# Seven late weight loads in a pairwise-product kernel: from SyncE's queue over sixteen DMA engines to GpSimd's queue over fourteen

## The chip, the cores and the metric

The kernel runs on one core of a Trainium2 chip. The core has TensorE (PE, with its weight loads as PEld), VectorE (DVE), ScalarE (ACT), GpSimd (POOL), SyncE (SP), and sixteen DMA engines that move data between HBM and the core's memory. The metric is device time in microseconds (us); the kernel before takes 754.85 us, the median of three runs (754.69 to 755.86).

## The reference

There are 1024 samples with 32 fields of 128 numbers each. Every pair of fields i < j (496 pairs) has a 128 x 128 matrix of its own:

```python
v_i = inputs[:, I_IDX, :]
v_j = inputs[:, J_IDX, :]
transformed = jnp.einsum('bpd,ped->bpe', v_i, W)
return transformed * v_j
```

All of it is float32. The output is 1024 x 496 x 128 numbers, 260 MB; the inputs are 17 MB of fields and 32 MB of matrices.

## The kernel before

**Layout and order.** The host transposes, so that the embedding dimension lies on the 128 partitions and the samples run along the free dimension. The pairs go from i = 30 down to i = 0, and for each i over j = i+1 to 31. A unit u is half a pair (512 samples); two units make a pair q, two pairs a chunk c, eight pairs one weight load (`WL`), four pairs one output group (`OG`). The order of all instructions on each engine is the order in which the Python loop over u (L215) writes them out; the scheduler doesn't move them. An engine that waits therefore holds up all that the loop wrote for it later.

**One unit.** The first 15 pairs use one float32 matmul each (L188). All others use three matmuls on split operands: the field and the matrix are each cut into a high part, a rest and a correction. `first(u)` issues two matmuls (L191) and a scaling of the result in PSUM by ACT (L192); three units later `second(u)` adds the third matmul (L200), and VectorE multiplies the result by field j into the output tile (L206). Eight PSUM tiles hold units in flight.

**Splitting.** For a chunk of two matrices ACT makes the high part (`wh`, L110), and GpSimd then makes `wl` and `wd` in three operations (L111 to L113). The same is done for each field in two halves (L125 to L131; for the first fields the last of these operations is VectorE's, L238). A chunk's split is written out three chunks ahead of its use and has four buffers. The list `todo` gives at most one such task a pair.

**Weights.** A weight load is one tile of 128 partitions by 4 KB (512 KB), three such tiles in turn (`WB`). Load c holds chunks 4c to 4c+3 and is issued on SP's queue (`load_w`, L98 to L101). It may start when the last split of load c-3, that of chunk 4c-9, has been read. Its place in the loop is pair 8c-17 (`w_at`, L158 to L162; 8c-11 for loads 55 to 57), but SP has next to nothing else to do and gets there early: it issues when the tile comes free.

**Fields.** Fields 17 to 31 have tiles of their own. Fields 1 to 16 lie in four tiles of 16 KB a partition (`g0` to `g3`), loaded four fields at a time by SP (L91 to L96). Field 0 comes late into one of the weight tiles.

**Output.** A group of four pairs fills one 16 KB tile, which ACT's queue stores as one DMA of 2 MB (L231). There are three such tiles of their own, and until their fields are loaded the four tiles `g0` to `g3` serve too (`out_tile`, L171 to L175). From the load of `g0`, at 473.6 us of the profile, on only the three are left. VectorE can't start a group before the store that last used its tile has landed. The last groups are stored in smaller pieces.

**Queues.** SP's queue carries the loads, ACT's queue the stores and four early loads. GpSimd issues no DMA.

Of the kernel before, what the change touches and what calls it, by code (L numbers as in the profile page):

```python
# [7 lines left out]
F32 = mybir.dt.float32  # L8
# [3 lines left out]
P = 128  # L12
# [5 lines left out]
WL = 8  # L18
# [9 lines left out]
XLEAD = 5  # L28

XG = 4  # L30
XWAIT = 12
OWAIT = 20
SLAG = 2
# [8 lines left out]
def kernel(  # L42
# [22 lines left out]
    nc = tc.nc  # L65
# [3 lines left out]
    xpool = ctx.enter_context(tc.tile_pool(name="x", bufs=1))  # L69
# [8 lines left out]
    def load_x(f, pieces=1, eng=None):  # L78
        if f == 0:

            t = rpool.tile([P, WL, P], F32, tag="w", name="x_0").rearrange("p q e -> p (q e)")
        else:
            t = xpool.tile([P, BT], F32, tag=f"x{f}", name=f"x_{f}")
        s = BT // pieces
        for k in range(pieces):
            (eng or nc.sync).dma_start(out=t[:, k * s : (k + 1) * s], in_=xt[f, :, k * s : (k + 1) * s])
        x_sb[f] = t

    w_raw = {}

    def load_group(k):  # L91
        t = xpool.tile([P, XG, BT], F32, tag=f"g{k}", name=f"x_g{k}")
        f = XG * k + 1
        nc.sync.dma_start(out=t, in_=xt[f : f + XG].rearrange("m d b -> (m d b)").rearrange("(d m b) -> d m b", m=XG, b=BT))
        for m in range(XG):
            x_sb[f + m] = t[:, m, :]  # L96

    def load_w(c, splits=(0, WL), eng=nc.sync):  # L98
        w_raw[c] = rpool.tile([P, WL, P], F32, tag="w", name=f"w_{c}")
        for a, b in zip(splits, splits[1:]):  # L100
            eng.dma_start(out=w_raw[c][:, a:b, :], in_=wt[c, :, a:b, :])  # L101

# [30 lines left out]
    nq0 = NATIVE * (NATIVE + 1) // 2  # L133
# [11 lines left out]
    todo.sort(key=lambda t: t[1])  # L145

    load_w(0, (0, 1, WL), nc.sync)
    load_x(NF - 2, pieces=2, eng=nc.scalar)
    load_x(NF - 1, pieces=2, eng=nc.scalar)
    load_x(NF - 3)  # L150
    load_x(NF - 4)
    load_w(1, eng=nc.sync)
    for f in range(NF - 5, NF - 4 - XLEAD, -1):
        load_x(f)
    load_w(2, eng=nc.sync)


    w_at = {}  # L158
# [4 lines left out]
    x_at = XAFTER * WL - 11  # L163
    assert x_at not in w_at and len(w_at) == NQ // WL - WB

    ngroup = NF // XG // 2
    group_at = {first_q[XG * k + XG + 1] - XWAIT: k for k in range(ngroup)}
    until = {f"g{k}": q - OWAIT for q, k in group_at.items()}
# [12 lines left out]
    def first(u):  # L181
        q, h = divmod(u, 2)
        i, c = pairs[q][0], q // WC
        r = slice(q % WC * P, (q % WC + 1) * P)
        s = slice(h * HB, (h + 1) * HB)
        po[u] = ppool.tile([P, HB], F32, tag="po", name=f"po_{u}")
        if q < nq0:
            nc.tensor.matmul(po[u], w_raw[q // WL][:, q % WL, :], x_sb[i][:, s], start=True, stop=True)  # L188
        else:
            for t in (0, 1):  # L190
                nc.tensor.matmul(po[u], w_s[c][t][:, r], x_s[i][t][:, s], start=t == 0, stop=t == 1)  # L191
            nc.scalar.mul(po[u], po[u], 1.0 + EPS)  # L192

    def second(u):
        q, h = divmod(u, 2)
        i, j = pairs[q]
        r = slice(q % WC * P, (q % WC + 1) * P)
        s = slice(h * HB, (h + 1) * HB)
        if q >= nq0:
            nc.tensor.matmul(  # L200
                po[u], w_s[q // WC][2][:, r], x_s[i][2][:, s], start=False, stop=True, skip_group_check=True
            )
        g, k = divmod(q, OG)
        if k == 0 and h == 0:
            ots[g] = out_tile(g)
        nc.vector.tensor_tensor(ots[g][:, k, s], po.pop(u), x_sb[j][:, s], ALU.mult)  # L206
        if q >= NQ - 2:
            stores.append((u + SLAG, out[g, :, k, s], ots[g][:, k, s]))
        elif g == 0 or q >= NQ - OG:
            if h == 1:  # L210
                stores.append((u + SLAG, out[g, :, k], ots[g][:, k]))
        elif k == OG - 1 and h == 1:
            stores.append((u + SLAG, out[g], ots[g]))

    for u in range(2 * NQ + LAG + SLAG):  # L215
        q = u // 2
        if u < 2 * NQ:
            i, j = pairs[q]
            if u % 2 == 0 and j == i + 1 and XG * ngroup < i - 2 - XLEAD:
                load_x(i - 2 - XLEAD)  # L220
            first(u)
            if u % 2 == 0 and q in group_at:
                load_group(group_at[q])
            if u % 2 == 1 and q in w_at:
                load_w(w_at[q])
            if u == 2 * x_at + 1:
                load_x(0)
        if LAG <= u < 2 * NQ + LAG:
            second(u - LAG)
        while stores and stores[0][0] <= u - LAG:  # L230
            nc.scalar.dma_start(*stores.pop(0)[1:])  # L231
        if u % 2 == 1:
            ready = [t for t in todo if t[0] <= q]
            if ready:
                ready[0][2](u)
                todo.remove(ready[0])
        while later and later[0][0] <= u:
            nc.vector.tensor_tensor(*later.pop(0)[1:], ALU.subtract)  # L238
# [30 lines left out]
```

## Time and profile before

| what | value |
|---|---|
| median of three runs | 754.85 us |
| the profiled execution | 755.86 us, of which the span from the first to the last instruction is 754.1 us |
| moved to and from HBM | 310.04 MB, mean 411 GB/s |
| TensorE, VectorE, ScalarE, GpSimd busy | 702.0, 655.1, 626.1, 593.8 us |
| mean granted TensorE clock | 0.988 |
| late weight loads (w_45 to w_61) | issued from 519.3 to 700.9 us, landed 9.7 to 11.7 us after issue |
| one store of 2 MB | median 13.3 us from issue to landing, x122 |

How to read it. The page divides the span in 40 slices of 18.9 us and gives for each the bytes moved, and the share of time for which each engine was busy. The chain of waits goes back from the last instruction, at each step to what released it. A row of the waits reads: who waited, for whom, total us, times, longest us. A row of the windows reads: start and end, length, then busy us and number of instructions for PE, PEld, DVE, ACT and POOL, the granted clock, the share of time in which the DMA engines had a packet in work, and GB/s. A row of DMA queues reads: packets, MB, share of the time of sixteen engines; q10 carries the stores, q1 the loads. Besides these views the trace holds, for every DMA, the times at which its sixteen parts completed.

### The profile page before, as it was taken

What the parts mean: (1) busy time and instruction counts of PE and PEld (TensorE: products, weight loads), DVE (VectorE), ACT (ScalarE), POOL (GpSimd) and SP (SyncE); (2) the same over time, 40 slices, a digit from 0 to 9 for tenths busy, and PEclk for the clock granted to TensorE, in tenths of its full rate; (3) what the DMA queues carried; (4) which work ended last, traced back from release to release, by engine and by line L of the source; (5) the groups of instructions that cost most, each with busy time, mean ns of one, the idle gap of its engine ahead of it and who ended that gap; (6) DMA issues with size and microseconds to landing.
All of it is one profiled execution on the core that took longest, in us unless ns stands there. A gap on an engine that the chain in (4) does not pass through costs nothing.

```text
span 754.1 us, 10925 instructions
## 1 busy us (share of the span) xinstructions
PE 702.0 (93%) x2946; PEld 553.7 (73%) x2946; DVE 655.1 (87%) x1012; ACT 626.1 (83%) x1256; POOL 593.8 (79%) x863
## 2 busy tenths in 40 slices
PE   7998999999999999988999997899999999999993
PEld 2576778777778778766787786687878777777782
DVE  3999999998999999778899887789888889888894
ACT  1198989998899889877898996788989898888892
POOL 1689999999999898885988885868787878796660
PEclk9999999999999999999999999999999999999997
DMA  9999999999999999999999998999999999999997
GB/s 350 420 424 428 389 405 393 428 426 428 430 417 428 428 427 428 427 421 423 419 417 399 430 402 347 370 426 429 421 422 427 404 425 411 420 409 415 421 398 313
DMA packets 31309, 310.04 MB, mean 411 GB/s; under 512 B 3472, under 2 KB 3600, under 8 KB 15120
## 3 DMA queue, kind: packets, MB, share of 16 engines
q10 hardware_dynamic: 19584, 261.10, 82.2%
q1 hardware_dynamic: 11664, 48.24, 16.6%
q8 instruction: 24, 0.39, 0.2%
q14 instruction: 37, 0.30, 0.1%
HBM read 49.28 MB, written 260.05 MB: 410 GB/s over the span
## 4 chain that ended last, share of the span: by engine, by line
PE 62%; DMA 19%; POOL 10%; DVE 5%; issue 1%; ACT 1%; DVEq 0%; SPq 0%; POOLq 0%; ACTq 0%
PE po L191 39%; PE po L200 19%; DMA out_dram<-ot 18%; DVE ot L206 5%; PE po L188 3%; POOL wl L111 3%; POOL xd L131 3%; POOL xl L126 2%; POOL wd L113 2%; POOL xl L127 1%; DMA x<-in_xt_dram 1%; POOL wd L112 1%; ACT po L192 0%; ACT wh L110 0%; DVE xd L238 0%
## 5 line engine op out<-in xcount | busy, mean ns | idle before, releaser
L192 ACT ACTIVATE po<-po 128x512 f32<-128x512 f32 x962 | 545.3, 583 | 93.5 <-PE po L191 51.5
L206 DVE TENSOR_TENSOR ot<-po,x 128x512 f32<-128x512 f32 x720 | 468.0, 687 | 65.2 <-DMA out_dram<-ot 28.9
L191 PE MATMUL po<-xl,wl 128*128 128x512 f32 x962 | 378.8, 394 | 19.9 <-POOL wl L111 18.6
L191 PE MATMUL po<-xh,wh 128*128 128x512 f32 x962 | 379.2, 394 | 13.6 <-DVE ot L206 12.9
L200 PE MATMUL po<-xd,wd 128*128 128x512 f32 x962 | 376.5, 392 | 1.8 <-DVE xd L238 0.9
L111 POOL TENSOR_TENSOR wl<-w,wh 128x256 fp32r<-128x256 f32 x241 | 180.8, 750 | 77.8 <-ACT wh L110 76.5
L191 PEld LDWEIGHTS po<-xl,wl 128*128 128x128 f32 x962 | 181.8, 189 | 65.4 <-POOL wl L111 26.8
L191 PEld LDWEIGHTS po<-xh,wh 128*128 128x128 f32 x962 | 181.6, 189 | 59.8 <-DVE ot L206 21.5
L200 PEld LDWEIGHTS po<-xd,wd 128*128 128x128 f32 x962 | 181.7, 189 | 41.0 <-ACT po L192 2.4
L113 POOL TENSOR_TENSOR wd<-wl,wd 128x256 fp32r<-128x256 f32 x241 | 177.9, 738 | 20.1
L206 DVE TENSOR_TENSOR ot<-po,x_g 128x512 f32<-128x512 f32 x272 | 170.8, 685 | 23.3 <-DMA out_dram<-ot 11.1
L112 POOL TENSOR_SCALAR wd<-wh 128x256 fp32r<-128x256 f32 x241 | 99.1, 411 | 20.3
L110 ACT ACTIVATE wh<-w 128x256 fp32r<-128x256 f32 x241 | 99.0, 411 | 7.2 <-DVE ot L206 5.4
L131 POOL TENSOR_TENSOR xd<-xh,xl 128x512 fp32r<-128x512 f32 x32 | 41.3, 1290 | 2.7
L126 POOL TENSOR_TENSOR xl<-x_g,xh 128x512 fp32r<-128x512 f32 x32 | 41.5, 1297 | 0.0
L126 POOL TENSOR_TENSOR xl<-x,xh 128x512 fp32r<-128x512 f32 x20 | 26.3, 1315 | 16.3 <-ACT xh L125 16.1
L127 POOL TENSOR_SCALAR xl<-xl 128x512 fp32r<-128x512 f32 x52 | 34.4, 662 | 4.6
L188 PE MATMUL po<-x,w 128*128 128x512 f32 x60 | 30.2, 661 | 4.7 <-DMA x<-in_xt_dram 4.7
L188 PEld LDWEIGHTS po<-x,w 128*128 128x128 f32 x60 | 12.2, 210 | 21.9 <-issue 14.4
L125 ACT ACTIVATE xh<-x 128x512 fp32r<-128x512 f32 x20 | 12.4, 628 | 12.1 <-DMA x<-in_xt_dram 11.9
L238 DVE TENSOR_TENSOR xd<-xh,xl 128x512 fp32r<-128x512 f32 x20 | 20.6, 1032 | 0.0
L125 ACT ACTIVATE xh<-x_g 128x512 fp32r<-128x512 f32 x32 | 20.2, 630 | 0.0
(5 smaller groups left out, 1.7 us busy)
## 6 DMA issues: line engine op xcount, KB each, us to landing
out_dram<-ot ACTq DMA_DIRECT2D x122, 2048.0 KB, 13.3
w<-in_wt_dram SPq DMA_DIRECT2D x61, 512.0 KB, 10.3
x_g<-in_xt_dram SPq DMA_DIRECT2D x4, 2048.0 KB, 18.5
x<-in_xt_dram SPq DMA_DIRECT2D x14, 512.0 KB, 9.8
out_dram<-ot ACTq DMA_DIRECT2D x6, 512.0 KB, 9.3
x<-in_xt_dram ACTq DMA_DIRECT2D x4, 256.0 KB, 6.0
out_dram<-ot ACTq DMA_DIRECT2D x4, 256.0 KB, 8.2
w<-in_wt_dram SPq DMA_DIRECT2D x1, 448.0 KB, 4.6
```

What stands on the lines that cost most here:

```text
L110: nc.scalar.mul(h, raw, 1.0 - 2.0**-13)
L111: nc.gpsimd.tensor_tensor(l, raw, h.bitcast(F32), ALU.subtract)
L112: nc.gpsimd.tensor_scalar(d, h.bitcast(F32), EPS, 1.0, ALU.mult, ALU.mult)
L113: nc.gpsimd.tensor_tensor(d, l.bitcast(F32), d.bitcast(F32), ALU.subtract)
L126: nc.gpsimd.tensor_tensor(l, x_sb[f][:, s], h.bitcast(F32), ALU.subtract)
L127: nc.gpsimd.tensor_scalar(l, l.bitcast(F32), 1.0 / EPS, 1.0, ALU.mult, ALU.mult)
L131: nc.gpsimd.tensor_tensor(d, h.bitcast(F32), l.bitcast(F32), ALU.subtract)
L188: nc.tensor.matmul(po[u], w_raw[q // WL][:, q % WL, :], x_sb[i][:, s], start=True, stop=True)
L191: nc.tensor.matmul(po[u], w_s[c][t][:, r], x_s[i][t][:, s], start=t == 0, stop=t == 1)
L192: nc.scalar.mul(po[u], po[u], 1.0 + EPS)
L200: nc.tensor.matmul(po[u], w_s[q // WC][2][:, r], x_s[i][2][:, s], start=False, stop=True, skip_group_check=True)
L206: nc.vector.tensor_tensor(ots[g][:, k, s], po.pop(u), x_sb[j][:, s], ALU.mult)
```

## The change

A weight load whose number is in `WAPART` is divided. Its first 112 partitions are issued by GpSimd, with the source arranged as fourteen shares of eight rows; the host rearranges these rows, so that the data lie where they did. The remaining 16 partitions go by SP as before. Each of the seven loads stands at its old place in the loop (pair 8c-17), on GpSimd's queue now. Three pairs later GpSimd issues a small transfer (`move_on`) that copies rows of 64 bytes into an otherwise unused tile `mark`, arranged in two shares; a first one of five shares is issued at pair 15, and the last has thirteen. The shares add up to 5 + 7 x 14 + 6 x 2 + 13 = 128. The other loads, the fields, the stores and all arithmetic stay.

```diff
+NE = 14
+ROWS = 8 * NE
+WAPART = (45, 47, 49, 51, 54, 58, 60)
+BACK = 3
...
+    mark = xpool.tile([32, 16], F32, tag="mark", name="mark")
+
+    def move_on(k):
+
+        nc.gpsimd.dma_start(out=mark[: 2 * k], in_=xt[0, : 2 * k, :16].rearrange("(b a) n -> a b n", a=k))
+
+    def load_apart(dst, src):
+        nc.gpsimd.dma_start(out=dst[:ROWS], in_=src[:ROWS].rearrange("(b a) m n -> a b m n", a=NE))
+        nc.sync.dma_start(out=dst[ROWS:], in_=src[ROWS:])
...
     def load_w(c, splits=(0, WL), eng=nc.sync):
         w_raw[c] = rpool.tile([P, WL, P], F32, tag="w", name=f"w_{c}")
+        if c in WAPART:
+            load_apart(w_raw[c], wt[c])
+            return
         for a, b in zip(splits, splits[1:]):
...
+    w_q = {c: q for q, c in w_at.items()}
+    back = []
...
             first(u)
+            if u == 2 * nq0:
+                move_on(5)
             if u % 2 == 0 and q in group_at:
                 load_group(group_at[q])
             if u % 2 == 1 and q in w_at:
                 load_w(w_at[q])
+                if w_at[q] in WAPART:
+                    back.append(q + BACK)
+            if u % 2 == 0 and q in back:
+                move_on(16 - NE if q < w_q[WAPART[-1]] else 13)
...
+    for c in WAPART:
+        wt[c, :ROWS] = wt[c, :ROWS].reshape(NE, 8, WL, P).transpose(1, 0, 2, 3).reshape(ROWS, WL, P).copy()
```

## The prediction

> **What bounds the kernel now.** I read the page first (busy shares, DMA by slice, chain), then the windows of the last third, where the change acts, then the waits in that third, then each DMA's completion times. The page says that two resources are nearly full at once.
>
> ```profile
> span 754.1 us, 10925 instructions
> PE 702.0 (93%) x2946; PEld 553.7 (73%) x2946; DVE 655.1 (87%) x1012; ACT 626.1 (83%) x1256; POOL 593.8 (79%) x863
> ...
> GB/s 350 420 424 428 389 405 393 428 426 428 430 417 428 428 427 428 427 421 423 419 417 399 430 402 347 370 426 429 421 422 427 404 425 411 420 409 415 421 398 313
> ...
> q10 hardware_dynamic: 19584, 261.10, 82.2%
> q1 hardware_dynamic: 11664, 48.24, 16.6%
> q8 instruction: 24, 0.39, 0.2%
> q14 instruction: 37, 0.30, 0.1%
> ...
> PE 62%; DMA 19%; POOL 10%; DVE 5%; issue 1%; ACT 1%; DVEq 0%; SPq 0%; POOLq 0%; ACTq 0%
> ```
>
> The best slices move 428 to 430 GB/s; those from the thirtieth on mostly 404 to 425. The first late load that the change touches (w_45) is issued at 519.3 us and the last load of all (w_61) at 700.9. The windows from 517 on, and the waits in 517 to 718, are:
>
> ```profile
> 517.00:718.00 201.00, 196.62 (x847) 157.13 (x846) 172.68 (x281) 180.08 (x361) 157.74 (x238) 1.00 1.01 418
> 718.00:754.10 36.10, 24.07 (x106) 19.37 (x104) 25.01 (x40) 21.38 (x41) 12.62 (x21) 0.89 0.85 354
> ```
>
> ```profile
> POOL wl L111 <- ACT wh L110: 30.0, 41, 1.4
> DVE ot L206 <- DMA out_dram<-ot: 14.1, 18, 1.5
> ...
> PEld po L191 <- DVE ot L206: 7.6, 16, 0.8
> ...
> PEld po L191 <- POOL wl L111: 3.9, 4, 1.5
> ```
>
> VectorE waits for an output tile's store to land, PSUM fills, and the weight loads of TensorE wait behind it: 7.6 us. At four field changes TensorE waits instead for GpSimd's split: 3.9 us. A group of four pairs (one 2 MB store) takes 5.73 us: the store issues at 517.34 and 717.80 lie 35 groups apart. Where nothing stalls it takes 5.4.
>
> The completion records say why the store is late. Each DMA completes in sixteen parts. For stores issued from 600 to 640 us the medians from issue are: first 7.1, eighth 7.4, third last 8.6, second last 8.7, last 12.1 us. For 490 to 520 us the last is at 11.1 and the eighth at 8.9; from 560 to 714 the gap between them stays at 4.5 to 4.9 us. So one engine of sixteen lags, its lag grows, and it levels off when the others run out of work. The instruction queue q8 fits it: 24 packets, one every 30 us; 0.2% of 16 x 754.1 us is 24 us, 1 us each, and the gap grows by about 1 us in 30 us (2.2 to 3.4 to 4.5 in 505 to 580 us). That q8 is all on one engine is inferred; the profile doesn't number engines.
>
> **The change, part by part.** The sum is made on the profiled execution: 755.86 us in all, 1.8 us of it outside the span. The median of the three runs is 1.0 us lower, and the sum is applied to that.
>
> *Work taken from two engines.* A load of 512 KB is 32 KB for each of sixteen engines. In the change seven loads (45, 47, 49, 51, 54, 58, 60) put 448 KB on fourteen engines, and the last 64 KB on all sixteen by SP. A left-out engine then moves 4 KB, the other fourteen 36. By the q10 row an engine moves 261.10 MB / (0.822 x 16 x 754.1 us) = 26.3 GB/s, so 28 KB are 1.09 us and 4 KB 0.16 us. Seven loads take 7.6 us from a left-out engine and add 1.1 to the others. As the lagging engine has work without a break from about 490 us to the end, 7.6 us is the ceiling if it is one of the two.
>
> *What the others leave open.* They become the limit. 418 against 428 GB/s over 201 us is 201 x (1 - 418/428) = 4.7 us of room, and at the end the last store lands at 7.2 us, its eighth part at 4.4: 2.8 us more. Less the 1.1 added: 6.4 us. TensorE could give 7.6 us (the row above). The least of the three counts: **-6.4 us**. What is late next: those fourteen engines need 2 MB / 16 / 26.3 = 5.0 us for a store and half of 1.25 for weights, 5.6 us a group against TensorE's 5.4, so waits for stores get shorter and don't vanish.
>
> *GpSimd's new issues.* Seven loads, seven small moves three pairs later, and one small move at pair 15, near 35 us: fifteen software issues on an engine that had none. No row has one. From below: SP's issue, 0.33 us (63 of 328 ns). From above: GpSimd's longest operation, 1.30 us (L126). I take the upper, since this is GpSimd's own work as L126 is. GpSimd is idle 201 - 157.7 = 43 us in the window, mostly waiting for ACT's wh (30.0 us), and fourteen issues are 18 us, so most hide there. They don't hide where a field is split (2 x (1.30 + 0.62 + 1.29) = 6.4 us of extra work), which is where TensorE waits for wl already. By the code a load by GpSimd stands behind the splits up to chunk 4c-7, while SP could issue after chunk 4c-9: two chunks, 2 x 2.7 = 5.4 us later. That puts w_47 at about 548 us and w_54 at 627.5, on the waits for wl at 548.1 and 627.5; the others fall clear of them. Queued behind the issue are wl, l and wd of the next chunks, and TensorE waits for those. Two issues at 1.3 us, with 0.6 recovered from the later wait for stores: **+2.0 us**; ends 0 (all covered) and 4 x 1.3 = 5.2 (the moves collide as well). The early move at 35 us lies where GpSimd is busy 21.8 of 30 us: nothing, at worst 1.3.
>
> *Later weights.* The issue comes twelve pairs ahead of the first split of its data, 12 x 1.36 = 16.3 us; loads land 9.7 to 11.7 us after issue in this window. Margin 4.6 us: nothing. With it gone, ACT would stop at wh with its evictions queued behind. GpSimd's new wait for the buffer is for wh and wl of a chunk split two chunks before on its own queue: nothing. SP keeps a 64 KB piece a load (16 packets): nothing, as SP is idle. The small moves read rows of 64 B, 60 in all (q1 and q10 move 31248 packets): nothing.
>
> Sum: -6.4 + 2.0 = -4.4 us, and 754.85 - 4.4 = **750.4 us**.
>
> *A rule against it.* The store and weight queues q10 and q1 together already fill 98.8% of sixteen engines' time. The Trainium skill, DMA: Bandwidth & Descriptors, section Rules for kernel authors, says that spreading DMAs over SP, ACT and GpSimd gives no bandwidth, since all run on the same sixteen engines. By it the gain is 0 and the sum 754.85 + 2.0 = 756.9. I keep the rows: the completions show one engine late and fifteen early, and the change takes work from an engine rather than adding a queue.
>
> *Which two.* Shares by the diff: 5, then seven times 14, six times 2, once 13: 128, eight rounds of sixteen. If shares go out in turn, the same two engines are left out each time and the next execution starts alike. That they are the late ones no row shows. The same page, section Why a DMA increments its semaphore by 16, says that a software DMA on k < 16 engines takes k consecutive ones from a round-robin cursor; from a cursor at 0 that leaves out engines 3 and 4, and nothing here shows whether these lag.
>
> **Rivals.** (1) *The left-out engines aren't the late one*, or the software queue divides otherwise. For it: nothing numbers the engines. Against: the shares come back to their start to the unit. The late engine gets 4 KB more in seven loads, +1.1 us, and GpSimd's issues, mostly under the waits for stores, 0.6: 756.6.
>
> (2) *GpSimd becomes the limit.* Place: the field changes, where its work runs end to end. Price: at p us an issue, with loads and moves both colliding at two places, 4p. From p = 1.6 us this outweighs the 6.4; at 2.5 us it is +10 - 6.4, so 758.5. For it: 3.9 us of waits there already, POOL busy in 78% of the window. Against: 43 us idle.
>
> (3) *The lag goes and the time stays.* Stores come earlier, but GpSimd's four stalls and 5.6 us a group on every engine set the pace: gain of the tail alone, 2.8 - 2.0 = 0.8, so 754.0. Against: the fast parts of a store land at 7.4 us, and a tile is needed again only two groups (10.9 us) after its store.
>
> **How the numbers follow.** Forecast 0.55, its own range 747.2 (the full 7.6) to 753; rival 1 0.15, rival 2 0.17, rival 3 0.13. The range 747.2 to 758.5 leaves out a part of rival 2 (two GpSimd issues dearer than 2.5 us) and little below. 0.2% is 1.5 us, about what a measurement tells from no change. Faster: nearly all of the forecast and a little of rivals 2 and 3, 0.57; within 0.2%: most of rival 3 and some of 1, 0.13; slower: rivals 1 and 2, 0.30.
>
> **What would show it.** Right: from about 600 us a store's last completion within 2 us of its eighth, the wait of VectorE for stores under half of 14.1 us, late slices above 420 GB/s, a shorter tail after the last store's issue. GpSimd's step: fifteen DMA issues on it with their durations, and PE's wait for wl near 6 us from 517 to 718. Wrong: the last completion still 4.5 us behind (rival 1), waits for wl of over 10 us (rival 2), or a wait of ACT's wh for weights that land over 16 us after issue. Before 517 us nothing should move, the waits for stores from 300 to 490 us included.

## The result and the profile after

| | us, median | range | runs |
|---|---|---|---|
| before | 754.77 | 754.33 to 755.86 | 4 |
| after | 751.38 | 750.17 to 751.70 | 4 |

The ratio is 0.995, with a 95% interval of 0.9933 to 0.9967: 3.4 us less, where 4.4 were forecast. The profiled execution after took 751.41 us, its span 749.6. Not all of the 4.4 us between the two spans (unrounded) belongs to the change. The 85th store is issued at 505.0 us before and 504.3 after, so 0.7 us were there already when the first changed load came; they are there at the first store of all (15.91 against 15.25 us). The other 3.7 us come after it.

The page after, with the lines that answer to those shown of before:

```profile
span 749.6 us, 10964 instructions
PE 700.9 (94%) x2946; PEld 552.6 (74%) x2946; DVE 653.9 (87%) x1012; ACT 627.3 (84%) x1256; POOL 602.4 (80%) x878
...
GB/s 344 423 430 426 410 424 404 424 430 427 427 410 425 430 427 431 424 417 423 415 413 401 429 403 324 361 430 426 422 403 423 421 425 412 412 427 427 427 426 360
...
q10 hardware_dynamic: 19584, 261.10, 82.6%
q1 hardware_dynamic: 10880, 45.03, 15.4%
q0 software_dynamic: 1264, 3.22, 1.2%
q8 instruction: 24, 0.39, 0.2%
...
PE 64%; DMA 18%; POOL 10%; DVE 4%; issue 1%; ACT 1%; DVEq 0%; ACTq 0%; POOLq 0%; SPq 0%
```

A new queue q0 carries 3.22 MB that q1 no longer carries. The last five slices move 427, 427, 427, 426 and 360 GB/s, where before they moved 409, 415, 421, 398 and 313: the engines are filled nearly to the end. The waits after, from 517 to 718 us (who, on whom: us in total, times, longest):

```profile
DVE ot L226 <- DMA out_dram<-ot: 9.7, 10, 1.9
...
PEld po L211 <- POOL wl L128: 5.2, 4, 1.6
...
PEld po L211 <- DVE ot L226: 2.4, 6, 0.7
```

L226, L211 and L128 are the lines L206, L191 and L111 of before. TensorE's weight loads now lose 2.4 us behind stores, in place of 7.6, and 5.2 us behind GpSimd's split, in place of 3.9. In the chain of waits from 517 to 718 us, stores have 25.1% before and no part after; TensorE has 91% of it. GpSimd's own rows in the groups of after show the price of an issue (count, busy us, mean ns):

```profile
L99 POOL DMA_DIRECT2D mark<-in_xt_dram x8 | 5.2, 648 | 0.0
L102 POOL DMA_DIRECT2D w<-in_wt_dram x7 | 4.4, 622 | 0.0
```

The completion records of the trace say whether the late engine caught up. Medians over the stores issued in each stretch, us from issue to the eighth, second last and last of sixteen completions:

| stores issued at | before | after |
|---|---|---|
| 490 to 520 us | 8.9, 10.4, 11.1 | 9.5, 11.1, 11.3 |
| 560 to 600 us | 7.5, 9.4, 12.0 | 9.5, 10.4, 11.6 |
| 600 to 640 us | 7.4, 8.7, 12.1 | 9.5, 10.7, 11.0 |
| 680 to 714 us | 7.5, 8.8, 12.1 | 10.2, 11.1, 11.4 |

Before, one completion stands 3.3 us or more behind all others from 600 us on. After, the last one stands 0.2 to 0.3 us behind the next there, and the eighth has moved up to 1.2 to 1.5 us below it. The others are fuller, and the late one is no longer alone.

### The profile page after: what moved, and what is told of

It reads as the page before. It is cut to its first block, busy times and chain, and to the rows that moved or that the text cites. A ratio compares the mean times of both kernels' runs of the same rounds, so it can differ in the third digit from the quotient of the medians.

```text
span 749.6 us, 10964 instructions
## 1 busy us (share of the span) xinstructions
PE 700.9 (94%) x2946; PEld 552.6 (74%) x2946; DVE 653.9 (87%) x1012; ACT 627.3 (84%) x1256; POOL 602.4 (80%) x878
## 3 DMA queue, kind: packets, MB, share of 16 engines
q1 hardware_dynamic: 10880, 45.03, 15.4%
q0 software_dynamic: 1264, 3.22, 1.2%
## 4 chain that ended last, share of the span: by engine, by line
PE 64%; DMA 18%; POOL 10%; DVE 4%; issue 1%; ACT 1%; DVEq 0%; ACTq 0%; POOLq 0%; SPq 0%
PE po L211 40%; PE po L220 20%; DMA out_dram<-ot 15%; DVE ot L226 4%; PE po L208 4%; DMA x<-in_xt_dram 3%; POOL xd L148 3%; POOL wl L128 2%; POOL xl L143 2%; POOL xl L144 1%; POOL wd L130 1%; POOL wd L129 1%; DVE xd L264 0%; ACT po L212 0%; ACT wh L127 0%
## 5 line engine op out<-in xcount | busy, mean ns | idle before, releaser
L226 DVE TENSOR_TENSOR ot<-po,x 128x512 f32<-128x512 f32 x720 | 465.9, 687 | 65.0 <-DMA out_dram<-ot 33.2
L211 PE MATMUL po<-xl,wl 128*128 128x512 f32 x962 | 378.7, 394 | 18.7 <-POOL wl L128 17.3
L211 PE MATMUL po<-xh,wh 128*128 128x512 f32 x962 | 379.2, 394 | 12.8 <-DVE ot L226 12.5
L128 POOL TENSOR_TENSOR wl<-w,wh 128x256 fp32r<-128x256 f32 x241 | 180.9, 751 | 66.0 <-ACT wh L127 63.6
L211 PEld LDWEIGHTS po<-xl,wl 128*128 128x128 f32 x962 | 181.5, 189 | 64.0 <-POOL wl L128 25.6
L211 PEld LDWEIGHTS po<-xh,wh 128*128 128x128 f32 x962 | 181.4, 189 | 60.1 <-DVE ot L226 21.8
L226 DVE TENSOR_TENSOR ot<-po,x_g 128x512 f32<-128x512 f32 x272 | 172.6, 686 | 20.9 <-PE po L220 9.3
L143 POOL TENSOR_TENSOR xl<-x,xh 128x512 fp32r<-128x512 f32 x20 | 26.3, 1313 | 15.7 <-ACT xh L142 15.4
L142 ACT ACTIVATE xh<-x 128x512 fp32r<-128x512 f32 x20 | 12.4, 627 | 11.4 <-DMA x<-in_xt_dram 11.3
(7 smaller groups left out, 11.2 us busy)
## 6 DMA issues: line engine op xcount, KB each, us to landing
w<-in_wt_dram POOLq DMA_DIRECT2D x7, 448.0 KB, 11.1
```

The costliest lines, as they stand in the source:

```text
L128: nc.gpsimd.tensor_tensor(l, raw, h.bitcast(F32), ALU.subtract)
L143: nc.gpsimd.tensor_tensor(l, x_sb[f][:, s], h.bitcast(F32), ALU.subtract)
```

## The experiments

All of them start from the kernel after. Each is compared with runs of the kernel before on the same chip, whose medians were 754.8 to 755.0 us.

**All sixteen engines by the same queue.** The cost of GpSimd's queue without anything left out:

```diff
-        nc.gpsimd.dma_start(out=dst[:ROWS], in_=src[:ROWS].rearrange("(b a) m n -> a b m n", a=NE))
-        nc.sync.dma_start(out=dst[ROWS:], in_=src[ROWS:])
+        nc.gpsimd.dma_start(out=dst, in_=src)
...
-                move_on(5)
+                move_on(16)
...
-                move_on(16 - NE if q < w_q[WAPART[-1]] else 13)
+                move_on(16)
...
-    for c in WAPART:
-        wt[c, :ROWS] = wt[c, :ROWS].reshape(NE, 8, WL, P).transpose(1, 0, 2, 3).reshape(ROWS, WL, P).copy()
```

> The seven late loads go whole by GpSimd's queue on all sixteen engines; the small transfers stay, with sixteen shares each, so GpSimd issues as many DMAs as in the changed kernel and no engine is left out. Theory (work taken from the late engine is the gain): the last completion of a store stays 4.5 us or more behind its eighth from 560 to 714 us, VectorE's wait for stores stays near 14 us, and the time is 754.8 plus 0 to 2 us for GpSimd. Rival (it is the other queue or the later issue that helps): about 751.4 us, as the changed kernel.

Measured: 755.96 us against 754.93, ratio 1.0014 (1.0005 to 1.0022). GpSimd's queue as a whole (fifteen issues, and what they do to other transfers) costs 1.0 us, and nothing of the gain is left. The waits of this kernel from 517 to 718 us:

```profile
DVE ot L225 <- DMA out_dram<-ot: 15.4, 19, 1.8
PEld po L210 <- DVE ot L225: 10.7, 16, 1.2
```

VectorE's wait is back at 15.4 us, and stores have 44.5% of the chain of waits in this stretch. TensorE's wait for GpSimd's split is 2.2 us here, under the 3.9 of before, so this profile doesn't show GpSimd's own time as the price. The lag from eighth to last is 3.2 to 3.7 us from 560 to 714 us, under the 4.5 that were expected: in part because the eighth itself comes later (8.2 to 9.1 us). So neither the queue nor the later issue helps by itself.

**Who is left out.** Three kernels differ from the one after by the number of shares in the first small transfer, and by the last one, which brings the sum back to 128. The edit with nine shares:

```diff
-                move_on(5)
+                move_on(9)
...
-                move_on(16 - NE if q < w_q[WAPART[-1]] else 13)
+                move_on(16 - NE if q < w_q[WAPART[-1]] else 9)
```

> As the changed kernel, but the first small transfer has nine shares in place of five and the last nine in place of thirteen, so that another two engines are left out. Theory (one certain engine is late, and the first transfer decides who is left out): the lag of 4.5 us or more stays, the late engine gets 7 x 0.16 us more, and the time is 755 to 757 us. Rival (any two engines do): 751.4 us.

> The first small transfer has four shares in place of five, the last fourteen in place of thirteen: the pair of left-out engines moves by one, and one of the two stays left out. Theory (one engine alone is late): either this kernel or the one with six shares keeps the whole gain, about 751.4 us, and the other one loses it, 755 to 757. Rival (both left-out engines are late ones): both kernels lie between, 752 to 754.

> The first small transfer has six shares, the last twelve: the pair moves by one the other way. Theory: the opposite of the kernel with four shares, 751.4 where that one is at 755 to 757 or the reverse. Rival: between, 752 to 754, like that one.

| first, last share | time, us | ratio (95%) | eighth and last completion, stores from 640 to 680 us |
|---|---|---|---|
| 5, 13 (after) | 751.38 | 0.9950 (0.9933 to 0.9967) | 10.6, 11.8 |
| 6, 12 | 752.01 | 0.9965 (0.9952 to 0.9977) | 10.5, 11.5 |
| 4, 14 | 757.42 | 1.0034 (1.0021 to 1.0047) | 9.0, 12.5 |
| 9, 9 | 757.55 | 1.0037 (1.0025 to 1.0049) | 9.1, 12.5 |

One small transfer of 64 byte rows, moved by one share, decides between 752 and 757.5 us. The waits from 517 to 718 us say the same, first for nine shares, then for six:

```profile
DVE ot L226 <- DMA out_dram<-ot: 15.0, 16, 2.0
PEld po L211 <- DVE ot L226: 11.6, 18, 1.5
```

```profile
DVE ot L226 <- DMA out_dram<-ot: 8.1, 7, 1.9
...
PEld po L211 <- POOL wl L128: 5.8, 4, 1.6
...
PEld po L211 <- DVE ot L226: 2.3, 3, 1.4
```

A start of five and of six share one of their two left-out engines if shares go out in turn; a start of four shares the other one with five. So one engine carries the lag, and the second one needn't have been left out. This is what the Trainium skill, DMA: Bandwidth & Descriptors, section Why a DMA increments its semaphore by 16 and not by 1, says of the round-robin cursor; the four kernels agree with it. Counted from a cursor at 0, the late engine would be number 4, but no run numbers the engines.

**Why that engine is late.** The traces also hold the start and length of every packet. In these records a packet often starts 4 ns before another one ends; read as the next packet of the same engine, some can be followed back. Before, the packet of 16 KB ahead of a store's last completion can be told for 13 of the 33 stores issued from 525 to 716 us: it took 625 to 644 ns in twelve of them. Ahead of the second last completion it can be told for 11, and took 611 to 613 ns in all. So the packets of the late engine take nearly 5% longer. With nine, with four and with sixteen shares such slow packets still end the stores (15 of 15, 12 of 15, 18 of 19 that can be told); with five and with six they seldom do (1 of 10, 1 of 13).

The instruction queue q8 isn't on that engine, as far as this can be told: the packet just ahead of one of q8 can be told for 10 of 24 before, and took 611 ns in all of them. An estimate from these lengths: 28 ns more (639, the median of the slow packets, against 611) for each of eight packets a store are 0.22 us in a group of 5.73 us, 1.2 us in 30 us, near the growth of the lag. What makes the engine slower, no run shows.

**Four loads in place of seven.**

```diff
-WAPART = (45, 47, 49, 51, 54, 58, 60)
+WAPART = (45, 49, 54, 60)
```

> The changed kernel with four loads apart (45, 49, 54, 60) in place of seven. Theory (the gain is the work taken from the late engine, less what the others get): 4 x 1.25 us less lag in place of 7 x 1.25; about half to three quarters of the gain, 752 to 753.2 us, the last completion 2 to 3.5 us behind the eighth around 600 to 700 us. Rival (as long as the lag is under some 3 us it costs nothing): 751 to 751.7 us, as with seven.

Measured: 754.13 us, ratio 0.9985 (0.9977 to 0.9994), over eleven runs from 751.98 to 755.48. Both expectations missed. Four sevenths of the work taken away gave one fifth of the gain. In its profile the last completion is still 3.2 to 3.9 us behind the eighth from 560 to 714 us, and in the waits from 490 to 718 us:

```profile
DVE ot L226 <- DMA out_dram<-ot: 26.6, 21, 2.4
PEld po L211 <- DVE ot L226: 12.1, 13, 1.9
```

That is more waiting than before had in the same stretch (15.4 and 7.6 us). So the gain doesn't grow evenly with the work taken away. Nor is it the slow engine that ends most stores here: the packet ahead of the last completion took 611 ns in 15 of 18 that can be told (stores issued from 525 to 716 us). Engines of full speed are late in its place, two of them: from 560 to 714 us the second last completion comes at 11.2 to 11.5 us here and at 9.9 to 11.5 in the kernel on all sixteen engines, where it came at 8.7 to 9.4 before. One reading is that GpSimd's queue adds some delay of its own; what delays these engines wasn't found.

**More issues by GpSimd.** Two more small transfers behind each, into the same tile:

```diff
                 move_on(16 - NE if q < w_q[WAPART[-1]] else 13)
+                for _ in range(2):
+                    move_on(16)
```

> The changed kernel with two more small transfers of sixteen shares behind each of the seven, so that GpSimd issues 29 DMAs in place of 15, of about 0.6 us each; who is left out stays the same. Theory (GpSimd's issues cost little, most of them lie in its idle time): 751.4 plus 0 to 1.5 us. Rival (GpSimd is close to the limit): 14 x 0.63 us more work costs 4 us or more, 755 or above.

Measured: 837.42 us, ratio 1.1087. Neither expectation had this. GpSimd's waits over the whole run, and its instructions in order of time around one of them (start, length):

```profile
POOL mark L99 <- DMA mark<-in_xt_dram: 66.8, 11, 7.6
...
POOL mark L99 <- DMA out_dram<-ot: 17.3, 3, 6.4
```

```profile
529.53 0.63 POOL L99 DMA_DIRECT2D mark<-in_xt_dram  x1
537.75 0.51 POOL L99 DMA_DIRECT2D mark<-in_xt_dram  x1 [7.58 <-DMA mark<-in_xt_dram]
544.62 0.51 POOL L99 DMA_DIRECT2D mark<-in_xt_dram  x1 [6.36 <-DMA out_dram<-ot]
545.14 0.74 POOL L128 TENSOR_TENSOR wl<-w,wh 128x256 fp32r<-128x256 f32 x1
```

Each transfer into `mark` waits for the landing of the one before it, 14 waits of 6.0 us each on average: 66.8 + 17.3 = 84.1 us, against 86.0 us lost to the kernel after (837.42 and 751.38). Three of them the profile puts down to a store; the code has them behind the same tile. All of GpSimd's splits stand behind them. In the kernel after the same dependence is there and costs nothing, since its late small transfers are 20 to 44 us apart and land in 7.4 to 9.2 us. So this run measured a wait, not issues. The same with three tiles:

```diff
-    mark = xpool.tile([32, 16], F32, tag="mark", name="mark")
+    marks = [xpool.tile([32, 16], F32, tag=f"mark{n}", name=f"mark_{n}") for n in range(3)]
...
+                for n in (1, 2):
+                    move_on(16, n)
```

> The kernel with two more small transfers behind each of the seven, again, but each of the three copies into a tile of its own, so that none waits for the landing of the one before it: 29 issues by GpSimd of 0.5 to 0.65 us each. Theory (the 82 us were the waits for landing, 14 of about 6 us, and the issues themselves mostly lie in GpSimd's idle time): 751.4 plus 0 to 2 us. Rival (GpSimd's time itself is the price): 14 x 0.55 = 7.7 us more, 757 or above.

Measured: 752.25 us, ratio 0.9969 (0.9959 to 0.9979). Fourteen more issues of about 0.5 us are 7 us of GpSimd's time. They cost 0.9 us by the medians of this kernel and the one after, 1.4 by their ratios (0.9969 and 0.9950), which overlap. The theory holds, and GpSimd waits nowhere for a landing in this trace: most of the 7 us lies in idle time.

**Earlier loads too.** The completions of before lag most from 300 to 440 us (eighth 8.3, last 16.8 us), which the change doesn't touch. Four kernels put earlier loads apart as well; the edit of the third:

```diff
-WAPART = (45, 47, 49, 51, 54, 58, 60)
+WAPART = (24, 27, 30, 33, 36, 39, 42, 45, 47, 49, 51, 54, 58, 60)
```

> Ten earlier loads (15, 18, ... 42) go apart as well, with their small transfers. Theory (the lag of one engine is also what stalls the kernel from 294 to 490 us, where the last completion is 8.5 us behind the eighth and PE's weight loads wait 13.9 us for VectorE from 300 to 490): the lag there falls under 2 us, most of that wait goes, and the time falls to 744 to 748 us. Rival (the stalls there come from the three remaining tiles and the 2 MB field loads, and GpSimd, which is the limit near fields' changes, pays for twenty more issues): 750 to 754 us.

> Seven earlier loads (30, 32, ... 42) go apart as well. Theory (the lag that has built up by 300 us is worked off by about 400): the waits from 390 on go, those from 294 to 345 us stay, 746 to 749 us. Rival: 750 to 754, as in the kernel from load 15 on.

> Seven earlier loads (24, 27, ... 42) go apart besides the seven late ones: as many issues as in the kernel from load 30 on, but one load in three, starting some 75 us earlier. Theory (the late engine falls behind by about 1 us in 30 us, so one load in three, 1.25 us each 38 us, keeps the lag from growing and a start before it is large is better): 746.5 to 749 us. Rival (where the loads are denser the lag is worked off sooner, before the stalls near 440 us): 749 to 751.

> Nine earlier loads (24, 26, ... 36, 39, 42) go apart besides the seven late ones. In the kernel with one load in three from 24 on the last completion is still 5.9 us behind the eighth from 300 to 440 us. Theory (that rest of the lag still costs): under 3.5 us of lag there, and 742 to 745.5 us. Rival (the rest costs nothing, GpSimd pays for four more issues): 745.5 to 748 us.

| earlier loads apart | time, us | range | ratio (95%) |
|---|---|---|---|
| 15, 18, ... 42 | 750.04 | 747.4 to 751.3 | 0.9931 (0.9916 to 0.9946) |
| 30, 32, ... 42 | 748.83 | 747.2 to 752.2 | 0.9927 (0.9910 to 0.9943) |
| 24, 27, ... 42 | 745.95 | 744.5 to 747.3 | 0.9884 (0.9870 to 0.9899) |
| 24, 26, ... 36, 39, 42 | 749.68 | 746.3 to 755.4 | 0.9926 (0.9899 to 0.9952) |

Of the waits from 300 to 490 us, first before, then with one load in three from 24 on:

```profile
DVE ot L206 <- DMA out_dram<-ot: 24.2, 14, 6.0
...
PEld po L191 <- DVE ot L206: 13.9, 6, 4.5
PE po L191 <- DVE ot L206: 11.7, 5, 4.1
```

```profile
DVE ot L226 <- DMA out_dram<-ot: 16.9, 11, 4.3
...
PEld po L211 <- DVE ot L226: 10.6, 8, 2.8
...
PE po L211 <- DVE ot L226: 7.2, 6, 2.4
```

The kernel after had 26.9, 17.7 and 11.5 us in these three rows. With 24, 27, ... 42 the time is 9 us less than before and 5.4 less than after, the best of all kernels here, a little under what the theory gave. The rows are of its fastest run. 30, 32, ... 42 comes at the theory's upper end. The other two are slower than their theories gave: the one from 15 on lies in the rival's range, the dense one above both ranges. Taking more from the late engine didn't help further. With loads from 15 on its lag is 1.4 us from 200 to 300 us, as meant, and the time is still 4 us above the best. The dense one spreads over 9 us from run to run, and its profiled execution is its slowest; what decides between a good and a bad execution stays open.

## Why the prediction was right, and where it was off

**What bounds the kernel: right, but for the cause of the lag.** One engine of sixteen was late, and what stalled VectorE and TensorE from 517 us on was its part of each store. The four starts show it: same bytes, same queue, same instructions, and 5.4 to 6.2 us between leaving out the right engine and another. The prediction put the lag down to the instruction queue q8, as an inference. The packet lengths speak against it: those of the late engine are 625 to 644 ns where others are 611, and q8's packets follow packets of 611.

**Work taken from two engines: right in kind, one engine would do.** That five shares at the start leave out the late engine followed from no row, and the prediction says so. If shares go out in turn, two of the sixteen starts leave out a given engine: five and six did, four and nine didn't. That it was hit is luck as far as the prediction shows, and by that count missing it was far likelier than the 0.15 that was given.

**What the others leave open, -6.4 us: mis-sized.** The step's own value is the kernel after less the one on all sixteen engines, each against its own before: -3.4 - 1.0 = -4.4 us. The 2.8 us counted for the end were too much: the last store lands at 6.1 us after issue, not 4.4, since the fourteen engines are behind by more than they were. In the two profiled executions that tail gave 7.2 - 6.1 = 1.1 us, which is 1.7 of the missing 2.0. The prediction had taken the fast engines' lead as free room and hadn't asked what they still hold when the last store comes.

**GpSimd's new issues, +2.0 us: 1.0 measured, for the queue as a whole.** How much of the 1.0 is GpSimd's time isn't separated. An issue takes 0.62 to 0.65 us, half of what was taken from L126. Nor did two of them collide with the waits at the field changes: they were placed at 548 and 627.5 us and came at 550.2 and 629.5, behind the late `wl` that TensorE waited for instead of ahead of it. An issue stands in the queue behind the same splits that are late there. The two errors, 2.0 and 1.0 us, have opposite signs, so the sum is off by 1.0 only; that they half cancel is luck.

**Later weights, nothing: right.** The seven loads land 10.9 to 12.7 us after GpSimd's issue, inside the 16.3 us, and ACT nowhere waits for weights in that window.

**The small moves, nothing: right, but its cover wasn't named.** Only the distance between them hides a wait for landing of 6 us each, with all of GpSimd's queue behind it.

**What would show it.** Last completion within 2 us of the eighth: yes. Late slices above 420 GB/s: from 656 us on (the thirty-sixth slice). PE's wait for wl near 6 us: 5.2. VectorE's wait for stores under half of 14.1: no, 9.7; but TensorE felt less of it, 2.4 in place of 7.6. A shorter tail: yes, by 1.1 us. Nothing moved before 517 us: not quite; VectorE's wait for stores from 300 to 490 us is 26.9 us in place of 24.2, in one execution each.

**The rivals.** The first had its mechanism right and its price low: leaving out the wrong two gives 757.4 and 757.6 us, where 756.6 stood; over the kernel on all sixteen engines that is 1.5 to 1.6 us for the 1.1 us of added work. The second, GpSimd as the limit, would have begun at 1.6 us an issue; 0.65 is far from it. The third, the lag gone and the time kept, is excluded by the result. The rule weighed against the change, that another queue gives no bandwidth, is borne out by the kernel on all sixteen engines (755.96), and doesn't touch the change, which takes work from one engine.

## What to carry to other kernels

When every DMA spreads evenly and the mean of the engines looks full, look at the sixteen completions of one transfer: if one is always late, look at the lengths of its packets too. Here the slowest engine set the pace, and moving one percent of its bytes off it was worth more than another queue. It has to be the right engine, and relief can be overdone: relieved earlier as well (one load in three) the kernel gained another 5.4 us; with nine and ten earlier loads apart in place of seven it kept only 1.7 and 1.3 of them. Before DMAs are issued from an engine that computes, look for every wait that the issue brings, also for a dummy destination that is written twice.

## What the runs showed that was not expected

- After waits of TensorE its granted clock falls to one half. Before, this happens at 343.5, 456.1 and 490.3 us, for 3.41 us each, around or just after waits of 2.8, 4.1 and 2.1 us, and once more when its work is done. The longest ends at 456.5 us, and the weight loads then follow each other at 427 ns in place of 226 until 459.6 us. The windows of before there (the granted clock is the third number from the end):

```profile
450.00:456.00 6.00, 2.35 (x11) 1.62 (x9) 0.29 (x1) 2.87 (x7) 3.72 (x6) 1.00 1.01 432
456.00:458.00 2.00, 1.54 (x4) 1.25 (x5) 2.00 (x4) 0.28 (x1) 0.00 (x0) 0.53 0.97 406
458.00:460.00 2.00, 2.00 (x7) 1.61 (x6) 1.97 (x4) 0.88 (x2) 0.00 (x0) 0.62 0.55 227
460.00:463.00 3.00, 3.00 (x14) 2.44 (x14) 2.05 (x5) 2.88 (x6) 1.15 (x2) 1.00 0.44 186
```

  The Trainium skill, TensorE: Matmul & The Clock Gate, section Part 1: The HAM clock gate, states a clock of one half after an idle window of about 3.4 us. The half clock agrees with the trace (0.53 and 0.62 in windows that hold some full speed too), but here waits of 2.1 and 2.8 us, shorter than such a window, were followed by it as well. A long wait for a store thus costs more than its own length, and the DMA engines run low behind it: 227 and 186 GB/s.

- Which engines a DMA of GpSimd's queue uses carries over from one transfer to the next: a transfer of ten rows of 64 bytes near 31 us decides who is left out of a load 490 us later.
